# Moving a row gather from the end of one image's token selection into the middle of the next image's attention

## The chip, the core and the metric

The kernel runs on one core of one Trainium2 chip. The metric is the device time of one launch in microseconds; the time before is the median of three runs. A trace of one further, profiled execution is at hand, with all instructions, semaphore events and DMA packets.

## The reference, cut to what matters

64 images of 256 x 256 go through a Fourier neural operator (four layers, the "tokenizer"). The rows of the result, 256 tokens of width 256, together with 77 text tokens make 333 tokens per image. They go through one attention and then through a feed-forward that only processes a part of the tokens:

```python
h = tokenizer(x)                                # [64, 256, 256]
h = concat([h, txt], axis=1)                    # [64, 333, 256]
h = h + attention(layernorm(h))
x = layernorm(h)                                # what the feed-forward gets
weights = x @ wr + br                           # one number per token
idx = top_k(weights, 166)[:165]                 # the tokens that are processed
sel = take_along_axis(x, idx)                   # their rows
y = (gelu(sel @ w1 + b1) @ w2 + b2) * weights[idx]
h = h + (zeros.at[idx].set(y) + x)
```

So 165 of the 333 rows of each image are picked by rank, gathered, processed and put back.

## The kernel before, in words

The first three quarters of the time compute the four Fourier layers of all images; nothing there is touched. The last stage takes the images one after the other. The feature maps of the last layer lie in DRAM, 8 MB per image.

The functions of the last stage, each called once per image:

- `image_rows(b)` (L889) makes the image's token rows `h`. Eight loads of 1 MB (`ch`, L909, issued by SyncE, a pool of seven buffers) feed 32 matmuls (L911), which accumulate in one PSUM tile `hp` after L899 and L904. ScalarE moves `hp` to `h` (L916); the text rows are loaded into the same tile (L917).
- `attention(b, h)` (L1000): layer norm and transposes (L933, L943, `azT`), query matmuls (L1006), scores (L1018), softmax, values (L1032), transposes of the probabilities (L1047), the output matmuls (L1056), the residual `h1` (L1059, with the bias that GpSimd has added to `h`, L1052). A second layer norm gives `z` (named `fz` in the profile), which GpSimd writes to a DRAM tensor (L1064), one of three in turn.
- `select(b, z)` (L947): the weight of each token (L955), spread over all partitions by matmuls with a diagonal matrix `dg` (L960). VectorE counts for each token how many others rank before it (L970 to L979) and builds a 0/1 matrix `place` from rank and token (L982). Then come the lines that the change moves: six small matmuls (L991, 12 records in the profile) of `place` with the token numbers give a list `who`, cast by VectorE (L994), of 83 and 82 tokens; two indirect DMAs of GpSimd (L995) fetch those rows of `z` from DRAM to the tile `zr`.
- `feed_forward(b, ...)` (L1067): transposes of `zr` (L1074), moved to `zs`; 32 + 32 matmul records (L1082, L1093) with a gelu in between (L1086); transposes back (L1103); GpSimd writes the result to DRAM (L1106), fetches it back by rank with three indirect DMAs (L1110, tile `o`) and adds `z` to `h1` (L1113).
- `finish(b, ...)` (L1116): scale and residual on VectorE (L1119), and 17 stores to the output by GpSimd (L1124, L1128).

The order of the work is that of the tile framework's scheduler, which interleaves what the program gives it; each engine then runs its own list strictly in that order, and waits for semaphores. The program hands over, for each image `b`: the rows of image `b+2`, the attention of `b+1`, the finish of `b-1`, the feed-forward of `b`, the selection of `b+1`:

```python
for b in range(B):
    now = done
    if b + 2 < B: hs[b + 2] = image_rows(b + 2)
    if b + 1 < B: done = attention(b + 1, hs.pop(b + 1))
    if last: finish(b - 1, *last)
    last = feed_forward(b, *now)
    if b + 1 < B: done += select(b + 1, done[1])
```

The DMAs of GpSimd use eight semaphores in turn; an issue waits until the DMA eight issues earlier has landed. In one image GpSimd's list reads: three bias adds (L1052), three writes of `z` (L1064), three adds (L1113), two writes of the feed-forward's result (L1106), three gathers (L1110), three stores (L1124), the first gather of rows (L995), one store, the second gather, the remaining 13 stores.

On TensorE the list of an image reads: L1074, L1082, L1093, L1103 mixed with L960, the first L991, L899, L943, L904, L911 with the other L991 strewn in, L1006, L1018, L1032, L1047, L1056.

Of the kernel before, what the change touches and what calls it, by code (L numbers as in the profile page):

```python
# [138 lines left out]
def tile_fno_fusion_transformer(ctx: ExitStack, tc: tile.TileContext, a, cst_d, grid_d, out):  # L139
# [35 lines left out]
    def evict(dst, src, act_every=3):  # L175

        flip[0] += 1
        if act_every and flip[0] % act_every == 0:
            nc.scalar.copy(dst, src)
        else:  # L180
            nc.vector.tensor_copy(dst, src)  # L181
# [695 lines left out]
    def psum():  # L877
        return pp.tile([128, 512], F32, name="pp")
# [68 lines left out]
    def select(b, z):  # L947


        wcol = small.tile([128, 3], F32, name="wcol")  # L950
        ps = psum()
        for t in range(3):
            r = rows[t]
            junk = tp.tile([128, TOK], F32, name="junk", bufs=1)
            nc.vector.scalar_tensor_tensor(  # L955
                junk[:r, :D], z[:r, t, :], 1.0, wrB[:r], ALU.mult, ALU.mult, accum_out=wcol[:r, t:t + 1]
            )
            dg = tp.tile([128, 128], F32, name="dg")
            nc.vector.tensor_scalar(dg[:r, :r], ID[:r, :r], wcol[:r, t:t + 1], None, ALU.mult)
            nc.tensor.matmul(ps[:, toks[t]], lhsT=ONES[:r], rhs=dg[:r, :r], start=True, stop=True)  # L960
        wrow = tp.tile([128, TOK], F32, name="wrow")
        nc.vector.tensor_scalar(wrow, ps[:, :TOK], brB, None, ALU.add)
        fw = small.tile([128, 3], F32, name="fw")
        idx = small.tile([128, 3], U32, name="idx")
        place = tp.tile([128, 3, KEPT], F32, name="place")
        for t in range(3):
            r = rows[t]
            junk = tp.tile([128, TOK], F32, name="junk", bufs=1)
            wc = small.tile([128, 1], F32, name="wc")
            nc.vector.scalar_tensor_tensor(  # L970
                junk[:r, :r], wrow[:r, toks[t]], 1.0, ID[:r, :r], ALU.mult, ALU.mult, accum_out=wc[:r]
            )
            gt = small.tile([128, 1], F32, name="gt")
            nc.vector.tensor_scalar(junk[:r], wrow[:r], wc[:r], None, ALU.is_gt, ALU.add, accum_out=gt[:r])
            eq = small.tile([128, 1], F32, name="eq")
            nc.vector.scalar_tensor_tensor(
                junk[:r], wrow[:r], wc[:r], TRI[:r, t, :], ALU.is_equal, ALU.mult, accum_out=eq[:r]
            )
            nc.vector.tensor_add(gt[:r], gt[:r], eq[:r])  # L979
            nc.vector.tensor_scalar(fw[:r, t:t + 1], gt[:r], float(KEPT), wc[:r], ALU.is_lt, ALU.mult)  # L980
            nc.vector.tensor_scalar(idx[:r, t:t + 1], gt[:r], float(KEPT), None, ALU.min)
            nc.vector.tensor_scalar(place[:r, t, :], IOTA[:r], gt[:r], None, ALU.is_equal)  # L982

        ps = psum()
        who = small.tile([128, 2], U32, name="who")
        zr = tp.tile([128, 2, D], F32, name="zr")
        for c, k in enumerate(kept):
            n = k.stop - k.start
            for t in range(3):
                r = rows[t]  # L990
                nc.tensor.matmul(  # L991
                    ps[:n, 2 * c:2 * c + 2], lhsT=place[:r, t, k], rhs=TOKN[:r, t, :], start=t == 0, stop=t == 2
                )
            nc.vector.tensor_copy(who[:n, c:c + 1], ps[:n, 2 * c:2 * c + 1])  # L994
            nc.gpsimd.indirect_dma_start(  # L995
                zr[:n, c, :], None, z_d[b % 3][:, :], bass.IndirectOffsetOnAxis(ap=who[:n, c:c + 1], axis=0)
            )
        return fw, idx, zr

    def attention(b, h):  # L1000
        z, zT = layer_norm(h, "a")
        qT = tp.tile([128, 2, TOK], F32, name="qT")
        for eh in range(2):
            ps = psum()
            for dh in range(2):
                nc.tensor.matmul(  # L1006
                    ps[:, :TOK], lhsT=wqk[:, dh, 128 * eh:128 * eh + 128], rhs=zT[:, dh, :],
                    start=dh == 0, stop=dh == 1,
                )
            nc.scalar.activation(qT[:, eh, :], ps[:, :TOK], AF.Identity, bias=bqk[:, eh:eh + 1], scale=1.0)  # L1010
        v = tp.tile([128, 3, D + 2], F32, name="v")
        p_ = tp.tile([128, 3, TOK], F32, name="prob")
        sm = small.tile([128, 3], F32, name="sm")
        for t in range(3):
            r = rows[t]
            ps = psum()
            for eh in range(2):
                nc.tensor.matmul(  # L1018
                    ps[:r, :TOK], lhsT=qT[:, eh, toks[t]], rhs=zT[:, eh, :], start=eh == 0, stop=eh == 1
                )  # L1020
            scale = 1.0 / D ** 0.5
            mx = small.tile([128, 1], F32, name="mx")
            nc.vector.reduce_max(mx[:r], ps[:r, :TOK], axis=AX.X)
            nc.vector.tensor_scalar_mul(mx[:r], mx[:r], -scale)
            nc.scalar.activation(
                p_[:r, t, :], ps[:r, :TOK], AF.Exp, bias=mx[:r], scale=scale, accum_out=sm[:r, t:t + 1]
            )
        for t in range(3):
            r = rows[t]
            ps = psum()  # L1030
            for dh in range(2):
                nc.tensor.matmul(  # L1032
                    ps[:r, :D + 2], lhsT=zT[:, dh, toks[t]], rhs=wvE[:, dh, :], start=dh == 0, stop=dh == 1
                )
            nc.vector.tensor_add(v[:r, t, :], ps[:r, :D + 2], bvE[:r])
            nc.vector.reciprocal(sm[:r, t:t + 1], sm[:r, t:t + 1])

            for n in range(2):
                nz = small.tile([128, 1], F32, name="nz")
                nc.vector.tensor_scalar(nz[:r], v[:r, t, D + n:D + n + 1], 0.0, None, ALU.not_equal)  # L1040
                nc.vector.tensor_mul(sm[:r, t:t + 1], sm[:r, t:t + 1], nz[:r])
        pT = tp.tile([128, 3, TOK], F32, name="probT")
        for jt in range(3):
            r = rows[jt]
            ps = psum()
            for t in range(3):
                nc.tensor.transpose(ps[:r, toks[t]], p_[:rows[t], t, toks[jt]], ID[:rows[t], :rows[t]])  # L1047
            evict(pT[:r, jt, :], ps[:r, :TOK], 2)
        h1 = tp.tile([128, 3, D], F32, name="h1", bufs=3)
        for t in range(3):  # L1050
            r = rows[t]
            nc.gpsimd.tensor_add(h[:r, t, :], h[:r, t, :], boB[:r])  # L1052
            ps = psum()
            for jt in range(3):
                rj = rows[jt]
                nc.tensor.matmul(  # L1056
                    ps[:r, :D], lhsT=pT[:rj, jt, toks[t]], rhs=v[:rj, jt, 0:D], start=jt == 0, stop=jt == 2
                )
            nc.vector.scalar_tensor_tensor(  # L1059
                h1[:r, t, :], ps[:r, :D], sm[:r, t:t + 1], h[:r, t, :], ALU.mult, ALU.add  # L1060
            )
        z = layer_norm(h1, "f")
        for t in range(3):
            nc.gpsimd.dma_start(z_d[b % 3][128 * t:128 * t + rows[t]], z[:rows[t], t, :])  # L1064
        return h1, z

    def feed_forward(b, h1, z, fw, idx, zr):  # L1067

        zs = tp.tile([128, 2, KEPT], F32, name="zs")
        ps = psum()  # L1070
# [45 lines left out]
    def finish(b, o, h1, fw):  # L1116
        for t in range(3):
            r = rows[t]
            nc.vector.scalar_tensor_tensor(  # L1119
                o[:r, t, :], o[:r, t, :], fw[:r, t:t + 1], h1[:r, t, :], ALU.mult, ALU.add  # L1120
            )
        for g in range(4):
            for n in range(4):
                nc.gpsimd.dma_start(  # L1124
                    out[b, 64 * n + 16 * g:64 * n + 16 * g + 16].rearrange("(p t) d -> p t d", t=2),
                    o[32 * g + 8 * n:32 * g + 8 * n + 8, 0:2, :],
                )
        nc.gpsimd.dma_start(out[b, S:TOK], o[0:TXT, 2, :])  # L1128

    hs = {n: image_rows(n) for n in range(min(2, B))}  # L1130
    done = attention(0, hs.pop(0))
    done += select(0, done[1])
    last = None
    for b in range(B):
        now = done
        if b + 2 < B:
            hs[b + 2] = image_rows(b + 2)
        if b + 1 < B:
            done = attention(b + 1, hs.pop(b + 1))
        if last:  # L1140
            finish(b - 1, *last)
        last = feed_forward(b, *now)
        if b + 1 < B:
            done += select(b + 1, done[1])
    finish(B - 1, *last)
# [33 lines left out]
```

## Time and profile before

| what | value |
|---|---|
| median of three runs | 12778.78 us (12762.29 to 12785.3) |
| the profiled execution's own time | 12773.36 us |
| its span | 12771.5 us |
| mean granted TensorE clock | 0.937 of full speed |
| busy, share of the span: TensorE, VectorE, ScalarE, GpSimd | 88%, 70%, 47%, 16% |
| last stage, 10000 to 12500 us: TensorE busy in 500 us | 439 to 442 us |
| same, moved by DMA | 209 to 222 GB/s |

The page gives shares over the whole span; for a change in the last stage they are of little use, as most of the span belongs to the Fourier layers. The stage is read from views with a window: the waits (who waited for whom, in total), the timeline of one engine (each line is a start, a duration, the instruction, its count, and in brackets the idle time before it and what ended it), and a table of stretches with the busy time of each engine, the granted clock and the share of time in which the 16 DMA engines were busy. Matmul records come in pairs[...].

### The profile page before, as it was taken

To read this page: it belongs to the slowest core of one execution; us is meant where nothing else is said; L and a number is where in the kernel's file an instruction comes from. 1 tells how busy PE (TensorE), PEld (TensorE's weight loads), DVE (VectorE), ACT (ScalarE), POOL (GpSimd) and SP (SyncE) were. 2 spreads that over 40 slices of the span, in tenths; PEclk is the share of its full clock that TensorE was granted. 3 is DMA by queue.
4 is the path that set the end of the run, shared out by engine and by line. 5 is a ranking of instruction groups with operands and counts; after the bars stand their busy time and mean duration, and the time that the engine had idled before them with its cause. 6 is when DMAs were issued, how large, how long until landed. Compare 5 with 4: busy or idle time off the path is not lost. (4 is left out here: it accounts for less than half of the span.)

```text
span 12771.5 us, 404517 instructions
## 1 busy us (share of the span) xinstructions
PE 11291.5 (88%) x181142; PEld 5846.3 (46%) x181142; DVE 8934.2 (70%) x10892; ACT 6056.8 (47%) x10153; POOL 2048.5 (16%) x2630
## 2 busy tenths in 40 slices
PE   6999999997999999999789999999996888888887
PEld 3444444443444444444344444444443555555555
DVE  6777777776777777777677777767775666666665
ACT  5555555555555555555455555555552323333332
POOL 0000000001000000000100000000002444544445
PEclk8999999998999999999989999999997889888898
DMA  6555555556989899989889998988987666556664
GB/s 226 203 201 199 202 200 204 198 201 222 362 347 353 347 354 348 353 343 353 308 338 350 350 354 344 354 344 342 356 347 248 216 214 220 209 210 219 220 221 143
DMA packets 648775, 3550.84 MB, mean 278 GB/s; under 512 B 136633, under 2 KB 187321, under 8 KB 248057
## 3 DMA queue, kind: packets, MB, share of 16 engines
q1 hardware_dynamic: 539520, 3392.85, 69.7%
q0 software_dynamic: 100368, 128.39, 3.8%
q8 instruction: 1417, 23.22, 0.7%
q10 hardware_dynamic: 7144, 3.72, 0.1%
q14 instruction: 326, 2.66, 0.1%
HBM read 1794.51 MB, written 1729.56 MB: 276 GB/s over the span
## 5 line engine op out<-in xcount | busy, mean ns | idle before, releaser
L669 ACT ACTIVATE ring<-ring 128x1024 f32<-128x1024 f32 x3072 | 3108.8, 1012 | 1191.5 <-PE ring L662 1156.2
L650 DVE STREAM_TRANSPOSE t<-vo 128x2048 f32<-128x2048 f32 x1536 | 3550.4, 2311 | 174.1 <-ACT vo L645 12.9
L662 PE MATMUL ring<-vo,w 32*32 32x512 f32 x49152 | 2854.1, 623 | 384.6 <-DVE zt L689 138.9
L645 ACT ACTIVATE vo<-ring 128x1024 f32<-128x1024 f32 x1536 | 1569.8, 1022 | 2986.2 <-PE ring L638 2372.3
L646 DVE TENSOR_SCALAR vo<-ring 128x1024 f32<-128x1024 f32 x1536 | 1859.4, 1211 | 601.5 <-PE ring L638 410.5
L679 PE MATMUL ring<-t,cst 32*32 32x512 f32 x49152 | 1861.2, 601 | 308.5 <-issue 307.0
L689 DVE STREAM_TRANSPOSE zt<-ring 128x1024 f32<-128x1024 f32 x384 | 711.6, 1925 | 1661.6 <-PE ring L679 1661.6
L597 POOL TENSOR_TENSOR ams<-am,sk 48x512 f32<-48x512 f32 x384 | 487.4, 1269 | 8634.2 <-DMA am<-mix 8229.4
L662 PEld LDWEIGHTS ring<-vo,w 32*32 32x32 f32 x49152 | 762.6, 104 | 1894.1 <-ACT ring L669 481.1
L679 PEld LDWEIGHTS ring<-t,cst 32*32 32x32 f32 x49152 | 971.6, 103 | 1161.5 <-issue 707.6
L638 PE MATMUL ring<-vin,ws 32*32 32x512 f32 x32768 | 1235.7, 606 | 20.2 <-issue 17.3
L911 PE MATMUL hp<-ch,win 128*32 128x512 f32 x4096 | 685.5, 713 | 1.1 <-DMA ch<-v 1.1
L1124 POOL DMA_DIRECT2D out_dram<-o x1024 | 537.4, 531 | 914.9 <-DMA zr<-zr,who 741.3
L702 PEld LDWEIGHTS ring<-cst,zt 128*128 128x128 f32 x4608 | 534.9, 193 | 176.2 <-ACT vo L645 160.0
L669 ACT ACTIVATION_READ_ACCUMULATOR ring<-ring 128x1 f32 x3072 | 584.3, 190 | 0.0
L702 PE MATMUL ring<-cst,zt 128*128 128x96 f32 x4608 | 567.1, 280 | 7.6 <-DVE zt L689 7.6
L638 PEld LDWEIGHTS ring<-vin,ws 32*32 32x32 f32 x32768 | 253.1, 103 | 404.5 <-issue 373.6
L608 PE MATMUL ring<-ams,cst 49*128 49x512 f32 (+1 forms) x1536 | 391.3, 620 | 37.3 <-POOL ams L597 27.0
L1082 PE MATMUL pp<-zs,w 128*128 128x165 f32 x2048 | 370.1, 348 | 36.7 <-DVE zs L181 19.9
L1082 PEld LDWEIGHTS pp<-zs,w 128*128 128x128 f32 x2048 | 354.1, 224 | 47.1 <-DVE zs L181 25.1
L422 PE MATMUL mps<-wm,xh 32*64 32x128 f32 (+1 forms) x4608 | 120.7, 373 | 201.9 <-ACT e L434 77.6
L1056 PE MATMUL pp<-v,probT 128*128 128x256 f32 (+3 forms) x1152 | 269.5, 387 | 33.2 <-DVE probT L181 16.3
(940 smaller groups left out, 12093.8 us busy)
## 6 DMA issues: line engine op xcount, KB each, us to landing
v<-vo SPq DMA_DIRECT2D x1536, 1024.0 KB
vin<-v SPq DMA_DIRECT2D x1024, 1024.0 KB
ch<-v SPq DMA_DIRECT2D x512, 1024.0 KB
mix<-ob SPq DMA_DIRECT2D x96, 512.0 KB
am<-mix SPq DMA_DIRECT2D x384, 96.0 KB
xin<-in_x_dram SPq DMA_DIRECT2D x16, 1024.0 KB
mv<-in_x_dram SPq DMA_DIRECT2D x256, 64.0 KB
zr<-fz POOLq DMA_DIRECT2D x128, 128.0 KB
```

The costliest lines, as they stand in the source:

```text
L638: nc.tensor.matmul(ps[n][32 * j:32 * j + 32], lhsT=ws[32 * n:32 * n + 32], rhs=v[32 * n:32 * n + 32, 2 * j:2 * j + 2, :], start=False, sto ...
L645: nc.scalar.activation(of[:, 0:2], t2[0], AF.Relu)
L646: nc.vector.tensor_scalar(of[:, 2:4], t2[1], 0.0, None, ALU.max)
L650: nc.vector.transpose(t32[b, t // 2][:, :, 8 * (t % 2):8 * (t % 2) + 8, :].rearrange("p y s c -> p s y c"), o.rearrange("p s (y l) -> p s ...
L662: nc.tensor.matmul(ps[n][32 * j:32 * j + 32], lhsT=w4[i + 1][32 * n:32 * n + 32], rhs=o[32 * n:32 * n + 32, 2 * j:2 * j + 2, :], start=Tru ...
L669: nc.scalar.activation(t2[n], t2[n], AF.Square, accum_out=acc[:, at:at + 1])
L679: nc.tensor.matmul(ps[n][32 * j:32 * j + 32], lhsT=FYT[32 * n:32 * n + 32, k, :], rhs=t32[b, j][32 * n:32 * n + 32, k].rearrange("p s c -> ...
L689: nc.vector.transpose(zt[:, h].rearrange("p k c -> p c k"), t2[h].rearrange("p n (s c) -> p c (n s)", c=C),)
L702: nc.tensor.matmul(ps[:, 0, 96 * g:96 * g + 96], lhsT=zt[:, h, k0:k0 + 4, :].rearrange("p k c -> p (k c)"), rhs=FX[:, h, 48 * r:48 * r + 9 ...
L911: nc.tensor.matmul(hp[32 * g:32 * g + 32], lhsT=win[:, 7 - t:39 - t], rhs=ch[:, g], start=False, stop=t == 7, skip_group_check=True,)
L1082: nc.tensor.matmul(ps[:, :KEPT], lhsT=w1[:, dh, 128 * hb:128 * hb + 128], rhs=zs[:, dh, :], start=dh == 0, stop=dh == 1,)
L1124: nc.gpsimd.dma_start(out[b, 64 * n + 16 * g:64 * n + 16 * g + 16].rearrange("(p t) d -> p t d", t=2), o[32 * g + 8 * n:32 * g + 8 * n + 8 ...
```

## The change

The second half of `select` becomes a function of its own, `fetch(b, place)`: the six matmuls of `place` with the token numbers, the two casts to `who`, the two indirect DMAs to `zr`. `select` returns the matrix `place` instead of the rows. `attention` takes a function `between` and calls it after its query matmuls have been handed over; the loop gives it the fetch of image `b` while attention works on image `b+1`. The last image, which has no attention after it, fetches directly before its feed-forward.

```diff
             nc.vector.tensor_scalar(place[:r, t, :], IOTA[:r], gt[:r], None, ALU.is_equal)
+        return fw, idx, place
+
+    def fetch(b, place):
 
         ps = psum()
         who = small.tile([128, 2], U32, name="who")
...
                 zr[:n, c, :], None, z_d[b % 3][:, :], bass.IndirectOffsetOnAxis(ap=who[:n, c:c + 1], axis=0)
             )
-        return fw, idx, zr
-
-    def attention(b, h):
+        return zr
+
+    def attention(b, h, between=None):
         z, zT = layer_norm(h, "a")
...
             nc.scalar.activation(qT[:, eh, :], ps[:, :TOK], AF.Identity, bias=bqk[:, eh:eh + 1], scale=1.0)
+        if between:
+            between()
         v = tp.tile([128, 3, D + 2], F32, name="v")
...
-    def feed_forward(b, h1, z, fw, idx, zr):
+    def feed_forward(b, h1, z, fw, idx, place, zr):
...
     for b in range(B):
-        now = done
+        now, got = done, []
         if b + 2 < B:
             hs[b + 2] = image_rows(b + 2)
         if b + 1 < B:
-            done = attention(b + 1, hs.pop(b + 1))
+            done = attention(b + 1, hs.pop(b + 1), lambda: got.append(fetch(b, now[-1])))
+        else:
+            got.append(fetch(b, now[-1]))
         if last:
             finish(b - 1, *last)
-        last = feed_forward(b, *now)
+        last = feed_forward(b, *now, *got)
```

## The prediction

> **What bounds the kernel now.** I read the page first (busy shares, slices), then the waits of the last stage (10000 to 12500 us), then the timelines of TensorE, GpSimd and SyncE over two images, then the granted clock by 4 us windows. The change touches only the last stage, from about 9780 us to the end: 64 images, one after the other, 46.8 us each (mean distance of the first L1082 matmul of successive images, first 61 distances). TensorE is busy some 88% there; the rest is two waits per image:
>
> ```profile
> PE pp L991 <- DVE place L982: 160.2, 53, 3.0
> ...
> PE pp L1074 <- DMA zr<-zr,who: 68.6, 54, 3.3
> ...
> POOL out_dram L1124 <- DMA zr<-zr,who: 669.2, 108, 10.4
> ```
>
> Columns: total us, times, longest. The first is 3.0 us in each image: TensorE has finished L960 and its next instruction is the first selection matmul L991, whose place matrix VectorE is still computing. The second is 1.3 us on average: the fetched rows arrive late. One image of the TensorE timeline (start, duration, count, idle time before):
>
> ```profile
> 11062.79 0.45 PE L960 MATMUL pp<-dg,cst 77*128 77x77 f32 x2
> 11066.27 0.44 PE L991 MATMUL pp<-cstt,place 128*83 128x2 f32 x2 [3.04 <-DVE place L982]
> 11066.64 1.06 PE L899 MATMUL pp<-cstt,a 48*32 48x256 f32 x2
> ...
> 11068.80 2.07 PE L904 MATMUL hp<-cst,y 32*128 32x256 f32 x4
> 11070.80 1.92 PE L911 MATMUL hp<-ch,win 128*32 128x512 f32 x2
> ...
> 11077.60 1.92 PE L911 MATMUL hp<-ch,win 128*32 128x512 f32 x16
> ```
>
> The last line is L911 at full clock, 0.12 us each. The lines before it are slower because the wait also costs clock (us, PE, PEld, DVE, ACT, POOL busy, PEclk, DMA share, GB/s):
>
> ```profile
> 11062.00:11066.00 4.00, 1.24 (x10) 0.96 (x8) 3.15 (x15) 0.77 (x2) 1.06 (x2) 1.00 0.15 42
> 11066.00:11070.00 4.00, 3.73 (x12) 2.39 (x13) 3.53 (x13) 0.36 (x1) 2.56 (x3) 0.51 0.11 33
> 11070.00:11074.00 4.00, 4.00 (x15) 1.01 (x17) 3.47 (x16) 0.00 (x0) 1.52 (x3) 0.50 0.38 102
> ...
> 11094.00:11098.00 4.00, 3.41 (x18) 2.52 (x16) 2.47 (x7) 0.00 (x0) 1.03 (x2) 1.00 1.02 388
> 11098.00:11102.00 4.00, 3.34 (x23) 3.18 (x24) 2.15 (x6) 3.40 (x5) 3.42 (x7) 1.00 0.48 150
> ```
>
> After the 3 us of idling TensorE is granted half clock. The DMA share tells the other half: the image loads `ch` (8 x 1 MB) run as one burst, share 1.0, and end near 11099. They start only when L911 frees the first of seven buffers. SyncE and GpSimd:
>
> ```profile
> 11075.00 8.50 SPq L909 DMA_DIRECT2D ch<-v  x8
> ```
> ```profile
> 11078.17 2.04 POOL L995 DMA_INDIRECT zr<-zr,who  x1 [3.31 <-DVE who L994]
> 11080.21 0.55 POOL L1124 DMA_DIRECT2D out_dram<-o  x1
> 11081.07 1.46 POOL L995 DMA_INDIRECT zr<-zr,who  x1 [0.30 <-issue]
> ...
> 11098.37 2.78 POOL L1124 DMA_DIRECT2D out_dram<-o  x5 [3.30 <-DMA zr<-zr,who]
> ```
>
> So the gather's second half, issued 11081.1, lands about 11098.1: 17 us, all of it inside the burst. The loop that sets the period is: rows land, L1074, feed-forward, L960, wait for place, L911, loads start, rows land.
>
> **What the skill says.** (1) "DMA: Bandwidth & Descriptors", section on queues, rings and completion order: an SDMA engine round-robins between queues packet by packet. The trace agrees: in the burst the packet records of GpSimd's queue alternate with the 8 KB packets of the loads, one 4 KB packet of the gather each 0.46 us; a 4 KB packet by itself takes 0.16 us. (2) Same page, section on why a DMA adds 16 to its semaphore: the engines used are the largest k up to 16 that divides the slowest dimensions. 83 rows give 1, 82 rows give 2. The trace agrees: 83 rows run as 21 packets of 4 KB in single file, 82 rows at twice that rate. (3) "TensorE: Matmul & The Clock Gate", Part 1: after an idle window of about 3.4 us the array goes to half clock. The trace is harsher: waits of 3.0 us are mostly followed by 6.8 us or more at 0.5, and waits of 1.5 to 2.6 us before L1074 by 3.4 us.
>
> **The change, part by part.** The order of instructions in the changed kernel tells where things go. Times below are from the first L1082 matmul of an image; "before" are means over 61 images.
>
> Nothing is added or removed: 6 selection matmuls (12 records), 2 VectorE casts and 2 gathers per image. On TensorE they move from between L960 and L911 to behind the query matmuls of the next image. On GpSimd the gathers stand behind six L1124 stores instead of three and four: 3 x 0.53 us more in front, but the stores are issued before the indices exist, so nothing is paid; the stores behind still wait for the gather, as now. On VectorE the casts now stand behind the next image's BN statistics (L925), which wait for `h` (L916, some 0.7 us after L911 ends): due before the selection, cost 0. SyncE's order in this stage is kept, so its loads only follow L911.
>
> - L960 ends: before 11.7. It is 10.5 after a short wait for rows and 12.2 after a long one (cold clock); I take 12.2.
> - The 3.0 us wait goes. What is late next? L899's operand is computed an image ahead, and the azT transposes read rows done long ago. L899 starts at 12.2 (before 15.0).
> - L899, L943 and L904 took 3.8 with half clock. Their full-clock timeline durations give 2.2. L911 starts at 14.4 (before 18.8).
> - L911: 64 records x 0.12 = 7.7, ends 22.1 (before 30.4: half clock and the L991s in between). I cost the eighth load at nothing: it is issued about 1 us after L911 starts and is needed 6.7 us after; a load takes about 5.4 us. If that cover is gone, up to 1 us.
> - Loads start at 15.4 (before 21.9). Burst about 23.8 us as in the trace, so it ends at 39.2 (before 45.8).
> - Query matmuls (L1006) 2.4, to 24.5; then selection. Place was complete 9.4 us after L960; with azT (0.5), y (0.4) and L897 (1.9) before it at most 12.2, so 21.6 to 24.4: just hidden. If not, 1 us.
> - Casts, then GpSimd: gathers issued at 25.5 and 27.9 (before 25.6 and 28.5): the same place in the image!
> - The gather: its first packet came 5.6 us after issue, so 31.1. By 39.2 some 17.6 of 21 packets pass at 0.46; the other 3.4 at 0.17 need 0.6. With 0.3 to land: 40.1. The second half, 10.25 packets on each of two engines behind it, lands at about 41.1.
> - TensorE reaches the transposes at 22.1 + 14.4 (attention as before, 13.9, plus selection 0.5) = 36.5. So it now waits for rows about 4 us instead of 1.3. That wait takes the place of the one removed, and the cold clock after it is the 12.2 above.
> - Transposes end 41.4, next L1082 at 42.0. With 0.4 for the small covers: 42.4, against 46.8.
>
> Sum: 4.4 x 62 images = 273 us. The profiled execution took 12773.4 us (span 12771.5), so 12500; the median of the runs shown is 5 us above it: 12505.
>
> The price that no row shows is a gather half inside and half outside the burst. Fast end: it is done 0.5 us after the burst, 39.7, period 40.4: 6.4 x 62 = 397 us, 12380. Slow end: both halves need the full 17.4 us from issue, 45.3, period 46.2: -37 us, 12740. I take the packet count between them, since the records show the rate to depend on alternation.
>
> **Rivals.**
> - *Latency from issue.* In the profile the gathers took 15.5 to 16.2 and 17.0 to 18.4 us whatever their distance from the burst's start. For it: that constancy. Against it: all lay inside a burst, so none shows what happens after it. Period 46.2 to 46.8: 12740 to 12779, centre 12765, no change.
> - *The exposed gather* (slower). VectorE's longer queue before the place matrix makes TensorE wait 2 us at the selection in the middle of attention, gathers are issued at 30, and take the longest 18.4: landed 48.4, period 49.3, +2.5 x 62 = +155: 12935. It decides from the second half landing later than 45.9. For it: place has under 3 us of slack. Against it: the burst should have ended by 39.2.
> - *TensorE-bound.* The wait for rows stays small, as gathers speed up altogether: period about 40, 12360. Against it: burst and gather start are tied to L911 and the selection.
> - *The change does nothing*: excluded by the instruction order.
>
> **Chances.** Forecast, with the part of it that loses a microsecond here or there: 0.72. TensorE-bound 0.06. Latency from issue 0.10, of which a little over half falls within 0.2% (26 us, about what a measurement of this kernel can tell from no change). Exposed gather 0.12. Faster 0.81, same 0.06, slower 0.13. Range 12380 to 12740: the two ends of the gather's cost; it leaves out the slower case, most of no change and a part of TensorE-bound. The forecast's own range is 12400 to 12650.
>
> **What would show it.** Right: no L991-type wait on place; full clock from L960 to the end of L911; distance from L1082 to L911 near 14.4; waits for zr near 4 us per image, with 0.5 clock after them in the feed-forward; gather latency down to about 13 to 14 us. Wrong: gather latency still 17 us, a selection wait on place in mid-attention, L911 waiting for `ch`, or no half clock after the longer wait.

## The result, and the profile after

The changed kernel takes 12661.6 us (median of 4 runs, 12659.6 to 12665.1), the kernel before beside it 12775.7 us: ratio 0.9912, 95% interval 0.9895 to 0.9929. It is faster by 114 us where 273 us were forecast. The profiled execution has a span of 12660.2 us. An image now takes 44.65 us in place of 46.76, where 42.4 was forecast (the distance of the first feed-forward matmuls, L1082 before and L1087 after, as a mean over the inner 57 images of the last stage; the means below are taken so, except where a total of the waits view is divided by the images in its window, 56 here).

The waits of the last stage (10000 to 12500 us; total, times, longest), answering to those shown of before:

```profile
PE pp L994 <- DVE place L982: 241.3, 56, 6.8
DVE o L1124 <- DMA o<-yr,idx: 230.2, 133, 5.4
...
DVE o L1124 <- issue: 129.4, 34, 5.5
```

and of the kernel before:

```profile
DVE o L1119 <- DMA o<-yr,idx: 50.9, 77, 4.4
```

The wait of the selection for `place` has not gone. It has moved with the selection (L991 is L994 now) into the attention, and has grown from 3.0 to 241.3 / 56 = 4.3 us per image. The wait for the fetched rows (L1074, now L1079) is down from 1.3 to 0.3 us (16.4 us in 19 waits). And a line that was small before stands out: VectorE waits for `o`, the feed-forward's results gathered back (L1115), before it can scale them (L1124, in `finish`; L1119 before). The 34 waits that the view puts down to "issue" end within 0.2 us of the landing of a gather of `o`, so they belong to it: 359.6 / 56 = 6.4 us per image, against 50.9 / 53.5 = 1.0 before.

TensorE over one image:

```profile
11064.62 0.45 PE L960 MATMUL pp<-dg,cst 77*128 77x77 f32 x2
11065.00 0.61 PE L899 MATMUL pp<-cstt,a 48*32 48x256 f32 x2
...
11067.33 7.07 PE L911 MATMUL hp<-ch,win 128*32 128x512 f32 x64
...
11076.68 0.39 PE L994 MATMUL pp<-cstt,place 128*83 128x2 f32 x4
11082.33 0.44 PE L994 MATMUL pp<-cstt,place 77*83 77x2 f32 x2 [5.25 <-DVE place L982]
...
11098.29 0.45 PE L1079 MATMUL pp<-cst,zr 83*128 83x83 f32 x4
```

L960 to L911 runs without a gap, as forecast. The first four selection records pass; then TensorE stands for 5.25 us for the third part of `place`. At the transposes (L1079) there is no wait at all. VectorE in the same microseconds:

```profile
11072.45 0.55 DVE L974 TENSOR_SCALAR_CACHE_REDUCE junk<-wrow,wc 77x333 f32<-77x333 f32 x1
...
11077.57 0.48 DVE L1124 SCALAR_TENSOR_TENSOR o<-o,fw,h 128x256 f32<-128x256 f32 x1 [4.56 <-issue]
...
11079.22 0.48 DVE L1124 SCALAR_TENSOR_TENSOR o<-o,fw,h 128x256 f32<-128x256 f32 x1 [0.69 <-DMA o<-yr,idx]
...
11081.39 0.48 DVE L1124 SCALAR_TENSOR_TENSOR o<-o,fw,h 77x256 f32<-77x256 f32 x1 [1.62 <-DMA o<-yr,idx]
...
11081.97 0.29 DVE L982 TENSOR_SCALAR place<-cstt,gt 77x165 f32<-77x165 f32 x1
```

The three L1124 of the image before stand in VectorE's list between the steps of the last rank. Each waits for a gather of `o`, and `place` stands behind them. The bracket of the first says "issue", but what ends then is the landing of the first gather, at 11077.5. In the kernel before, the list had nearly the same order, with two of them ahead of it. But there the image loads started 21.8 us into the image, 6.6 us after the first `o` gather was issued. Now they start at 14.4, beside it (14.5). From the first issue to the end of the last packet the three gathers took 5.4 us before and take 11.0 us now (medians over the packet records). The clock pays as well (us, PE, PEld, DVE, ACT, POOL busy, PEclk, DMA share, GB/s):

```profile
11076.00:11080.00 4.00, 1.07 (x8) 0.67 (x6) 1.51 (x5) 1.58 (x2) 0.00 (x0) 0.97 0.98 319
11080.00:11084.00 4.00, 1.68 (x6) 1.11 (x6) 2.19 (x11) 0.43 (x2) 3.16 (x7) 0.50 1.00 409
11084.00:11088.00 4.00, 4.00 (x14) 2.77 (x13) 1.87 (x6) 1.57 (x2) 3.69 (x3) 0.50 1.02 423
```

So the first theory was: VectorE's wait for `o` holds up `place`, this costs 4.3 us and some half clock per image, and without it the forecast would have come true. It was half right.

### The profile page after: what moved, and what is told of

Same layout as the page of the kernel before. It is cut to its first block, busy times and chain, and to the rows that moved or that the text cites. A ratio compares the mean times of both kernels' runs of the same rounds, so it can differ in the third digit from the quotient of the medians.

```text
span 12660.2 us, 404578 instructions
## 1 busy us (share of the span) xinstructions
PE 11148.0 (88%) x181142; PEld 5823.2 (46%) x181142; DVE 8876.0 (70%) x10892; ACT 6048.8 (48%) x10153; POOL 2037.2 (16%) x2630
## 5 line engine op out<-in xcount | busy, mean ns | idle before, releaser
L650 DVE STREAM_TRANSPOSE t<-vo 128x2048 f32<-128x2048 f32 x1536 | 3549.9, 2311 | 174.9 <-ACT vo L645 14.4
L911 PE MATMUL hp<-ch,win 128*32 128x512 f32 x4096 | 469.0, 602 | 12.8 <-DMA ch<-v 12.7
L1023 PE MATMUL pp<-azT,qT 128*128 128x333 f32 (+1 forms) x768 | 411.5, 690 | 0.0
L1124 DVE SCALAR_TENSOR_TENSOR o<-o,fw,h 128x256 f32<-128x256 f32 (+1 forms) x192 | 92.7, 483 | 397.7 <-DMA o<-yr,idx 262.4
L994 PE MATMUL pp<-cstt,place 128*83 128x2 f32 (+3 forms) x768 | 110.3, 248 | 282.4 <-DVE place L982 264.2
L1087 PE MATMUL pp<-zs,w 128*128 128x165 f32 x2048 | 319.6, 316 | 41.2 <-DVE zs L181 24.5
```

What stands on the lines that cost most here:

```text
L650: nc.vector.transpose(t32[b, t // 2][:, :, 8 * (t % 2):8 * (t % 2) + 8, :].rearrange("p y s c -> p s y c"), o.rearrange("p s (y l) -> p s ...
L1023: nc.tensor.matmul(ps[:r, :TOK], lhsT=qT[:, eh, toks[t]], rhs=zT[:, eh, :], start=eh == 0, stop=eh == 1)
```

## The experiments

Each edit is made to the changed kernel unless it says otherwise. Means per image in us; "wait" is TensorE's; "rows used" is the end of the row transposes, "cold" the time at half clock. L960, `place` and the rows are counted from the image's first feed-forward matmul.

| kernel | time | period | L960 ends | `place` done | wait, `place` | wait, rows | rows used | cold |
|---|---|---|---|---|---|---|---|---|
| before | 12775.7 | 46.8 | 11.7 | 21.2 | 3.0 | 1.3 | 46.2 | 10.5 |
| after | 12661.6 | 44.7 | 10.7 | 27.4 | 4.3 | 0.3 | 44.0 | 8.8 |
| a_hold | 12822.8 | 47.1 | 12.7 | 22.4 | 0 | 7.1 | 46.5 | 9.6 |
| a_no_o | 12769.3 | 46.7 | 12.6 | 22.8 | 0 | 6.3 | 46.1 | 9.9 |
| b_no_loads | 12139.5 | 36.7 | 10.5 | 21.4 | 0.1 | 0.1 | 36.1 | 0.4 |
| c_even | 12786.6 | 47.2 | 10.5 | 27.3 | 4.4 | 0 | 46.6 | 10.8 |
| c_88_after | 12615.8 | 43.8 | 10.5 | 27.5 | 4.5 | 0 | 43.2 | 7.7 |
| c_88_before | 12724.1 | 45.7 | 10.5 | 20.4 | 3.0 | 0 | 45.1 | 8.4 |
| e_hold_warm | 12723.8 | 45.6 | 10.9 | 20.6 | 0 | 0.7 | 45.0 | 1.7 |
| d_hold_88 | 12224.6 | 37.4 | 10.9 | 20.6 | 0 | 0 | 36.7 | 0.8 |
| f_hold_88_before | 12656.6 | 44.4 | 10.6 | 19.3 | 3.0 | 0 | 43.8 | 7.7 |

The kernel before, timed beside them, took 12781 to 12784 us. The changed kernel once more in the last group (r_after) took 12656.7 us, ratio 0.9902 (0.9885 to 0.9918).

> The changed kernel once more, beside the others on one chip: 12640 to 12680 us if its place between the other runs (88 + 77 below it, L1124 held back above it) is not one of the chip.

It came as expected, so the order of the table is not one of chips.

**a_hold: L1124 behind the selection.** The weights `fw` of `finish` pass through an addition of 0 times the first row maximum of the next attention.

```diff
             nc.vector.reduce_max(mx[:r], ps[:r, :TOK], axis=AX.X)
+            if late is not None and t == 0:
+                held = small.tile([128, 3], F32, name="held")
+                for n in range(3):
+                    nc.vector.scalar_tensor_tensor(
+                        held[:rows[n], n:n + 1], mx[:rows[n]], 0.0, late[:rows[n], n:n + 1], ALU.mult, ALU.add
+                    )
+                late = held
...
```

> The changed kernel, but the scaling of the fetched outputs o (L1124) takes its weights through an addition that needs the first row maximum of the next image's attention, so on VectorE it can only come after place and after the selection; three tiny VectorE additions per image are extra, nothing is left out. Theory 1 (VectorE waits for the o gathers ahead of the last place matrix): the wait of the selection matmul on place falls from 4.3 us to under 1 us per image, with it the half clock after it; the row gathers are issued near 26 instead of 29.4 and 31.9 us after the image's first L1082 matmul, and some wait for the rows comes back; period 44.7 to about 42, 12480 to 12580 us. Theory 2 (VectorE simply has too much work ahead of place, whoever waits): the wait on place stays at 3 to 4 us, 12640 to 12680 us. Theory 3 (the landing of the rows sets the period anyway): the wait on place goes but the wait for the rows grows by as much, 12640 to 12680 us.

Measured: 12822.8 us, ratio 1.003 (1.0018 to 1.0042): slower than the kernel before, and 161 us slower than the changed kernel. The first half of theory 1 is right: `place` is done 9.7 us after L960 in place of 16.7, TensorE's wait for it is gone, the gathers are issued at 26.4 and 28.7 us. But the rows are used at 46.5, later than with the wait. In the waits of this run:

```profile
PE pp L1086 <- DMA zr<-zr,who: 378.4, 103, 6.6
```

and TensorE around the rows of one image (L1086 transposes them, L1094 is the feed-forward):

```profile
11066.04 4.42 PE L1068 MATMUL pp<-v,probT 128*128 128x256 f32 x18 [0.28 <-ACT probT L179]
11077.08 0.51 PE L1086 MATMUL pp<-cst,zr 83*128 83x83 f32 x2 [6.61 <-DMA zr<-zr,who]
11079.60 0.54 PE L1086 MATMUL pp<-cst,zr 82*128 82x82 f32 x2 [2.02 <-DMA zr<-zr,who]
11080.74 7.72 PE L1094 MATMUL pp<-zs,w 128*128 128x165 f32 x32 [0.60 <-DVE zs L181]
```

L1094 takes 7.72 us here and 4.76 us at full clock. Theory 3 holds in kind: TensorE comes early and waits 7.1 us for the rows. Its figure does not: 12640 to 12680 us were expected under it, and the time is over 140 us above that. From issue to landing the gathers of the rows took:

```profile
DMA to landing us min/median/max: 5.4/16.6/19.2
```

against 11.9 (median) in the changed kernel, where they were issued 3 us later. The two halves landed at 42.5 and 45.9 here, at 42.5 and 42.9 there: sooner issued, not sooner landed.

**a_no_o: nobody waits for o.** L1124 scales `h1` in place and `h1` is stored.

```diff
-                o[:r, t, :], o[:r, t, :], fw[:r, t:t + 1], h1[:r, t, :], ALU.mult, ALU.add
+                h1[:r, t, :], h1[:r, t, :], fw[:r, t:t + 1], h1[:r, t, :], ALU.mult, ALU.add
...
-                    o[32 * g + 8 * n:32 * g + 8 * n + 8, 0:2, :],
+                    h1[32 * g + 8 * n:32 * g + 8 * n + 8, 0:2, :],
```

> The changed kernel, but L1124 scales h1 in place of the gathered o, and h1 is stored: the o gathers are still issued, but nothing reads them (so the outputs leave out the feed-forward's result). The order on VectorE hardly changes and its busy time is the same; only the wait for the o gathers is taken away. Theory 1: the wait on place falls from 4.3 to under 1 us per image, 12480 to 12580 us. Theory 2 (too much work on VectorE): wait and time stay, 12640 to 12680 us.

Measured: 12769.3 us, in neither expected range. The wait for `place` is gone. VectorE's order is not quite kept: two L1124 stand ahead of the last `place` here, three in the changed kernel. That is 0.5 us less work, against a wait of 4.3, which speaks for the wait for `o` and against the work on VectorE (theory 2); b_no_loads below, with the order of the changed kernel, decides it. The time is again that of the late rows:

```profile
PE pp L1079 <- DMA zr<-zr,who: 336.5, 93, 8.9
```

That is 336.5 / 53.5 = 6.3 us per image. Though `place` is done 4.6 us earlier than in the changed kernel, the rows' gathers are issued at the same time, 29.3 and 31.9 us: at least in part because GpSimd's stores ahead of them wait for the `o` gathers to land (123.9 us in 86 waits), as its DMAs use eight semaphores in turn. So VectorE is not the only engine that can hand this delay on.

**b_no_loads: no burst.**

```diff
+    ch = inp.tile([128, 4, 2, S], F32, name="ch")
+    nc.sync.dma_start(ch.rearrange("p g r y -> p (g r) y"), src[0][:, 0])
...
-            ch = inp.tile([128, 4, 2, S], F32, name="ch")
-            nc.sync.dma_start(ch.rearrange("p g r y -> p (g r) y"), src[b][:, t])
```

> The changed kernel, but the image loads ch are left out: one block is loaded once and stands in for all (so the outputs are not those of the images). There is no burst of 8 MB per image. Theory 1 with the burst as the reason for the late o gathers: they land in 3 to 4.5 us instead of a median of 8.5, the wait on place falls under 1.5 us, rows land in under 9 us, TensorE is the bound: period 38.5 to 41 us, 12280 to 12430 us. If the o gathers are late for another reason (the queue of GpSimd, its stores): they still take about 8 us, the wait on place stays above 3 us, 12600 us or more.

Measured: 12139.5 us, period 36.7, below the expected 38.5. Both waits are 0.1 us, and the `o` gathers take 5.5 us from the first issue to the end of the last packet, as in the kernel before (5.4). VectorE's order around `place` is that of the changed kernel, with the same three L1124 ahead of it, so theory 2 is out. Both waits need the burst.

**e_hold_warm: work in place of the wait.** Why is a_hold slower than the changed kernel, if both wait for the same rows? TensorE waits for `place` in mid-attention in one and for the rows just ahead of the feed-forward in the other. Added to a_hold behind the last attention matmul:

```diff
+        ps = psum()
+        for n in range(16):
+            nc.tensor.matmul(ps[:, 0:D], lhsT=pT[:, 0, toks[0]], rhs=v[:, 0, 0:D], start=True, stop=True)
```

> The run with L1124 held back, with 16 matmuls of 128x256 (about 6 us at full clock) put behind the last attention matmul, whose results nobody reads: they fill the 7.1 us in which TensorE waits for the rows there. Nothing is left out, and 6 us of TensorE work per image are extra. Theory A with the clock as the reason why that run is slower than the changed kernel (waiting for the rows gives half clock in the feed-forward, which puts off the image loads and with them the next rows by 2 us): the feed-forward runs at full clock, L960 ends at 10.5 to 11 in place of 12.7, rows land 2 us earlier in the image, period 47.1 to 44.5 to 45.5, 12660 to 12730 us, faster than without the extra work. If the clock has no part in it: 12820 us or more.

Measured: 12723.8 us, ratio 0.9961 (0.9948 to 0.9973), in the range expected if the clock is the reason: 99 us faster than a_hold with 7 us more work in each image. The useless matmuls (L1076) end before the rows are missed, and the feed-forward (L1097) is at full clock:

```profile
11042.93 7.07 PE L1076 MATMUL pp<-v,probT 128*128 128x256 f32 x32
...
11050.51 0.36 PE L1089 MATMUL pp<-cst,zr 82*128 82x82 f32 x2 [0.37 <-DMA zr<-zr,who]
11051.40 4.76 PE L1097 MATMUL pp<-zs,w 128*128 128x165 f32 x32 [0.52 <-ACT zs L179]
```

L960 ends 1.8 us earlier (10.9 against 12.7), the rows are used 1.5 us earlier, the period is 1.5 us shorter. The half clock after the wait is thus a part of the loop: rows late, cold feed-forward, image loads late, next rows late. The Trainium skill, "TensorE: Matmul & The Clock Gate", Part 1, says that the array goes back to full clock after a busy window of about 3.4 us, and that these windows run free, that is, they do not start with the work. The trace agrees: in the image of a_hold shown above L1094 loses 7.72 - 4.76 = 3.0 us, that is some 6 us at half clock, between one window and two.

**The shape of the gather.** The other way at the rows: gathers that land sooner. The rule of the transfer engines cited in the prediction gives 83 rows one engine. c_even fetches 96 + 80 rows, some of them for nothing (the queues that its expectation speaks of are these engines).

```diff
-    kept = [slice(0, (KEPT + 1) // 2), slice((KEPT + 1) // 2, KEPT)]
+    kept = [slice(0, 96), slice(96, KEPT)]
...
+        nc.vector.memset(who, 0)
...
-                zr[:n, c, :], None, z_d[b % 3][:, :], bass.IndirectOffsetOnAxis(ap=who[:n, c:c + 1], axis=0)
+                zr[:96 - 16 * c, c, :], None, z_d[b % 3][:, :],
+                bass.IndirectOffsetOnAxis(ap=who[:96 - 16 * c, c:c + 1], axis=0),
```

> The changed kernel, but the 165 rows are gathered as 96 + 80 (11 rows twice fetched or empty) instead of 83 + 82, so that a gather can be spread over 16 queues of the transfer engines instead of 1 or 2; one small memset more, nothing is left out. If the time of a gather in the burst is the packets that stand in single file: its landing falls from 8 to 17 us to 6 to 9 us. The kernel's time hardly moves if the wait for the rows is now small (0.3 us per image): 12635 to 12665 us. If the landing of the rows still sets the period: 12450 to 12600 us.

Measured: 12786.6 us, above both expected ranges. The gathers land in 6.4 us (median), the wait for the rows is gone, and the kernel is 125 us slower than the changed one. Part of that is the edit's own: its memset of `who` must wait until the gather that read the buffer has landed, and it stands in VectorE's list between the row maxima of the attention:

```profile
11032.93 0.14 DVE L1031 TENSOR_SCALAR mx<-mx 128x1 f32<-128x1 f32 x1
11035.65 0.06 DVE L989 MEMSET who<- 128x2 uint32 x1 [2.58 <-DMA zr<-zr,who]
```

So the run says what the shape does to the landing, not what it does to the time. The next four runs use 88 + 77 rows, both multiples of 11, without a memset:

```diff
-    kept = [slice(0, (KEPT + 1) // 2), slice((KEPT + 1) // 2, KEPT)]
+    kept = [slice(0, 88), slice(88, KEPT)]
```

By that rule (the Trainium skill, "DMA: Bandwidth & Descriptors", section on why a DMA adds 16 to its semaphore) this is 11 engines for each. The kernel before already had a gather of 77 rows, the third of `o`; its packets there are 11 of 4 KB and 11 of 3 KB, in agreement.

> The changed kernel with the rows gathered as 88 + 77 and nothing else: the one-number edit, without the memset that the run with 96 + 80 had in VectorE's list. Rows land within 7 us of issue, near 37 us after the image's first feed-forward matmul, 6 us before TensorE comes for them. Theory A: no gain worth telling from the rows, since the wait on place (4.3 us) is what is left: period 43.5 to 44.7, 12590 to 12670 us. If the rows' landing alone set the end in the changed kernel: period 40 to 42, 12370 to 12500 us. If the landing of o, which the memset run left late, is helped too, the wait on place falls and the time lies between the two.

Measured: 12615.8 us, ratio 0.9875 (0.9861 to 0.989). TensorE does not wait for the rows; its wait for `place` (250.1 us in 55 times) and the period are as expected.

> The kernel before with the rows gathered as 88 + 77 and nothing else. It waits 3.0 us for place and 1.3 us for the rows per image, with half clock after each. Theory A: the wait for the rows and the half clock in the feed-forward go (L960 ends at 10.5 in place of 11.7), the wait for place stays: period 46.8 to between 43.5 and 45, 12580 to 12680 us. If the latency of the gather is no matter here: 12740 to 12780 us.

Measured: 12724.1 us, ratio 0.9956 (0.9943 to 0.9969). The wait for the rows goes and L960 ends at 10.5, as expected, but the gain is 1 us per image and not 2 to 3. The rest is taken back in the attention, which is 1.5 us longer (15.4 from the end of L911 to the transposes, 13.9 before). There GpSimd's bias addition (L1052) now falls on VectorE's tiny products (L1041):

```profile
11021.23 2.10 POOL L1052 TENSOR_TENSOR h<-h,boB 128x256 f32<-128x256 f32 x3
...
11021.92 1.44 DVE L1041 TENSOR_TENSOR sm<-sm,nz 128x1 f32<-128x1 f32 x1
...
11023.40 0.16 DVE L1041 TENSOR_TENSOR sm<-sm,nz 128x1 f32<-128x1 f32 x1
...
11024.60 1.57 PE L1056 MATMUL pp<-v,probT 128*128 128x256 f32 x6 [1.11 <-DVE probT L181]
```

1.44 us for an instruction of 0.15. It is so in 48 places of this run (1.0 to 2.5 us) and in none of the kernel before; these products take 1.3 us more per image in all. The Trainium skill, "SBUF — State Buffer", "SBUF: two separate sides", says of a VectorE instruction with two SBUF inputs and a GpSimd instruction that reads SBUF that the one that starts first has a shared port pair for its whole instruction and the other is blocked. The trace agrees that VectorE stands while GpSimd adds. But it stands longer than for the one addition in hand: an addition takes 0.7 us, and the product shown ends at 11023.36, with the last of the three (11023.33).

**d_hold_88: both waits taken away.**

> The run with L1124 held back, and the 165 rows gathered as 88 + 77 in place of 83 + 82; nothing is left out. In that run the wait for place was gone and the wait for the rows was 7.1 us per image, and the 96 + 80 gathers landed in 6.4 us where 83 + 82 took 13 to 17. Theory A (the two waits stand side by side: TensorE late at the selection, and rows that land late because they pass the transfer engines in single file inside the burst; either alone sets the end): with both gone TensorE does not wait at either place, feed-forward and attention run at full clock, period 38 to 41 us, 12250 to 12450 us. Theory B (something else holds the image at about 44 us, the image loads or the stores): 12600 us or more.

Measured: 12224.6 us, ratio 0.9566 (0.9554 to 0.9578), period 37.4, a little below what was expected. One image:

```profile
11028.29 0.56 PE L994 MATMUL pp<-cstt,place 128*88 128x2 f32 x6
...
11036.92 4.39 PE L1068 MATMUL pp<-v,probT 128*128 128x256 f32 x18 [0.28 <-ACT probT L179]
11041.15 0.45 PE L1086 MATMUL pp<-cst,zr 88*128 88x88 f32 x4
11042.36 4.76 PE L1094 MATMUL pp<-zs,w 128*128 128x165 f32 x32 [0.76 <-DVE zs L181]
```

Neither the selection nor the transposes wait, and the half clock is down to 0.8 us per image. The edits do not add up: a_hold alone loses 161 us to the changed kernel, 88 + 77 alone gains 46, both gain 437.

**f_hold_88_before: the same without the change.** The selection and the gathers go back between L960 and L911 of the image.

> The fastest run with the change itself undone: L1124 held back and the rows gathered as 88 + 77, but the selection and the gathers between L960 and L911 of the image, as in the kernel before; nothing is left out. Theory A (the change is what hides place, and the two edits are what lets it): the 3.0 us wait at L991 and the half clock after it are back, the wait for the rows is nil; period 43 to 45.7, 12560 to 12720 us, so that the change is worth 340 to 500 us here against 114 us by itself. If the two edits do it without the change: 12200 to 12300 us.

Measured: 12656.6 us, ratio 0.9903 (0.9886 to 0.9919), with 168.6 us in 56 waits for `place`, 3.0 us each. So the change is worth 12656.6 - 12224.6 = 432 us once the two things that hid it are gone, and 114 us by itself.

## Why the prediction was wrong in size

The direction and the mechanism at the start were right, step by step. L899 starts at 10.6 (forecast 12.2) and L911 at 12.9 (14.4) without a gap and at full clock; L911 ends at 21.0 (22.1); the loads start at 14.4 (15.4). All are early by 1 to 1.6 us, because the wait for the rows, which was forecast at 4 us with a cold feed-forward after it, is 0.3 us. Two terms failed, on two paths that lie side by side. Either alone loses most of what d_hold_88, where both waits are gone, gains on the kernel before timed beside it (559 us): with the wait for `place` alone (c_88_after) 168 us of gain are left, with the wait for the rows alone (a_hold) none. (A slip outside these terms: the first 61 distances average 46.7 us, not 46.8, which takes 6 us off the forecast.)

**"Place was complete 9.4 us after L960 ... at most 12.2, so ... just hidden. If not, 1 us."** It is complete 27.4 - 10.7 = 16.7 us after L960. It was not the work added to VectorE's list: without the wait for `o` it takes 9.7 us (a_hold, d_hold_88). The allowance up to 12.2 even counted some work twice, as azT stood ahead of the last `place` in every image of the kernel before, and L897 and y in about half of them. The term was read from a trace in which `o` lands before the burst; the same sum had moved the burst 6.5 us forward, and I did not ask what else was in flight there. SyncE's list is unchanged, but its loads now meet the `o` gathers, and on VectorE L1124 stands ahead of the last `place`. Instead of "at most 1 us" TensorE loses 8.1 us between the end of L911 and the transposes: 43.5 - 21.0 = 22.5 us against the forecast 14.4. Of these 4.3 are the wait. Most of the other 3.8 is half clock: TensorE is busy for 17.4 us of this stretch, 6.8 of them at half clock, against 14.1 and 0.1 in d_hold_88. a_hold, a_no_o and b_no_loads take the wait away in three ways. d_hold_88 needs 14.5 us there, so the forecast's own figure was right for an attention that does not wait.

**"Burst about 23.8 us as in the trace", with the rows landed at 40.1 and 41.1.** This fails by itself. a_hold is nearly the kernel that the prediction described (only the scaling and the stores of `o` come later), with `place` hidden and gathers issued at 26.4 and 28.7 (forecast 25.5 and 27.9), and its period is 47.1, not 42.4. Its rows land at 42.5 and 45.9, the last 4.8 us late. Loads issued 1.0 us later are the smallest part. From the first load's issue to the end of the burst's last packet is 29.0 us on average, 5.2 more than forecast (the kernel before already had 26.9), and the rows land 0.5 after it where 1.9 was forecast: 1.0 + 5.2 - 1.4 = 4.8. In the changed kernel the burst ends at 41.5 (27.1 us after the first issue) and the rows land at 42.9, 1.8 us later than forecast.

I had taken one burst's length from a table of 4 us stretches. That burst, issued at 11075.0, really ends at 11101.3, after 26.3 us. And I had counted the gather's packets as guests of the burst, which cost it nothing. But the 21 packets of the first half go in single file, 0.16 us each, which by estimate (21 x 0.16) takes 3.4 us of one engine that has its share of the 8 MB to move too. The row split alone shortens the burst from 29.0 to 27.8 us (a_hold to d_hold_88) and from 26.9 to 25.0 (before to c_88_before), though not in the changed kernel (27.1 and 27.3 in c_88_after). The end of a burst in a_hold (columns as above):

```profile
11072.00:11076.00 4.00, 0.00 (x0) 0.00 (x0) 0.00 (x0) 0.00 (x0) 0.00 (x0) 0.65 0.77 211
11076.00:11080.00 4.00, 0.91 (x4) 0.58 (x4) 0.00 (x0) 0.00 (x0) 0.68 (x2) 0.50 0.11 35
```

A DMA share of 0.11 is less than two of 16 engines, while TensorE waits for the rows and next to nothing computes. That the tail is the gather's engine is my reading; the records do not name the engine. That the shape of the gather is the cause of the late rows is shown by 88 + 77: in d_hold_88 the burst ends at 42.6, and TensorE finds the rows at 36.3.

**Why the result lies between.** In the changed kernel TensorE comes to the transposes at 43.5 and the rows have landed at 42.9: two paths of nearly equal length, one through VectorE's wait for `o`, one through the rows. So each single repair gains little. The wait for `place` even does some good where it stands: TensorE comes late enough to find the rows, the feed-forward is at full clock, and the next loads start 2 us earlier than in a_hold (14.4 against 16.4).

**The rivals.** "Latency from issue" was right about gathers that lie almost wholly in the burst: 16.6 us in a_hold. The argument against it, that the end of the burst would set it free, holds only for halves issued nearer that end: 13.2 and 10.9 us in the changed kernel. "The exposed gather" had the wait in mid-attention (2 us, was 4.3) and the issue (30 us, was 29.4 and 31.9) right; it failed with the second half's landing at 48.4, which came at 42.9. "TensorE-bound", forecast at a period of 40, is d_hold_88 at 37.4, after two more edits.

**Left open.** Why the first packet of an `o` gather comes 4.6 us after its issue when loads are in flight, and 2.0 without them; and what of the 125 us that c_even loses to the changed kernel is not its memset.

## What to carry to other kernels

When a step on the critical path becomes shorter, list everything that starts earlier because of it, and look up what was in flight in that place: here the image loads moved 7 us forward, into three small gathers that nobody had on the path, and an engine that works through its list in order handed the delay on. If removing one wait gains nothing, do not call it harmless: look for a second path of the same length, and remove both in one kernel (437 us together, -161 and +46 singly). Choose the number of rows of an indirect gather so that it has a large divisor up to 16, as 88 and 77 have in 11, and look at which instruction follows a wait of some microseconds on TensorE, since that one pays the half clock.

## What the runs showed of the hardware

- From the issue of a gather to its first 4 KB packet: 2.0 us with no loads in flight (the first `o` gather, before and in b_no_loads), 4.6 us with them (after), 5.4 (after) to 6.1 us (before) for the 83 rows. All are medians.
- In the burst, issue to landing is 16.6 us (median, a_hold) for 83 + 82 rows and 6.4 us (c_even) for 96 + 80, which move more bytes.
- 7 us of useless matmuls per image made a_hold 99 us faster.
- A VectorE product of 0.15 us took 1.0 to 2.5 us in 48 places of c_88_before, where it fell on GpSimd's additions.
- Waits of 3.0 us on TensorE (before, at `place`) were followed by half clock for 6.8 or 10.2 us in each of the inner 57 images.
